# Two-layer graph attention on one core: a row buffer of 41 rows in layer 2, first operands kept in its tail, and TensorE sums for layer 1's largest tile

## The chip, the cores and the metric

The kernel runs on one core of one Trainium2 chip. The metric is device time in microseconds (us) of one execution, the median of several. The engines in the tables are PE (TensorE matmul), PEld (TensorE weight load), DVE (VectorE), ACT (ScalarE), POOL (GpSimd) and SP (SyncE, which here only issues DMAs). All numbers are fp32.

## The reference

10000 nodes carry 768 values each (`x`); 170000 directed edges, 10000 self loops among them, are sorted by destination. Each graph convolution adds one more self loop per node, so that every loop counts twice. Cut to what is computed:

```python
def gat_conv(x, W, a_src, a_dst, bias, heads, concat):
    xl = (x @ W).reshape(n, heads, out_ch)
    e = leaky_relu(a_src_dot(xl)[src] + a_dst_dot(xl)[dst], 0.2)
    e = exp(e - segment_max(e, dst)[dst])
    alpha = e / (segment_sum(e, dst)[dst] + 1e-16)
    return segment_sum(xl[src] * alpha, dst) + bias      # heads joined

h  = relu(layer_norm(gat_conv(x, W1, ..., b1, 4 heads of 256), g1, be1))
h1 = h + (x @ Wr1 + br1)                                  # 1024 columns
h  = layer_norm(gat_conv(h1, W2, ..., b2, 1 head of 768), g2, be2)
out = layernorm(x + h + (h1 @ Wr2 + br2))                 # 768 columns
```

So each node needs, in each layer, a weighted sum over the projected rows of all its neighbours, between two and some forty of them, and then norms and a product that belong to the node alone.

## The kernel before, in words

**Tiles and slots.** A first stage (lines 591 to 659, until about 940 us) multiplies `x` by W1 and writes a row for each node to `table1` in DRAM: 1024 products, four destination and four source logits, and the node's rank. At the same time it sorts the edge lists. The nodes are ordered by degree and cut into 79 tiles of 128. `TURNS` (L97) sets the order in which tiles are handled: every second one, from few neighbours to many, and then the others back down. By position in that order, as the text numbers tiles throughout, tile 0 has 8 rows, the next ones 10, 11, 12, 12, 13, 13, 14; tiles 22 to 24 have 18, 25 to 28 have 19, 29 to 31 have 20, 35 has 22, 38 has 26; tile 39 has 41 and is the largest; then come 27, 25, 24, 23, 22, 22, 21, 21, 20 (tiles 48 to 50), 19 (51 to 53), 18, and so on down to 9 rows in tile 78. A "row" of a tile is the k-th neighbour of each of its 128 nodes: one indirect gather of 128 table rows. There are 1377 rows in each layer. The first row of a tile is the nodes' own, and in layer 2 a plain DMA issued by SP (L452), since table2 is written in the tiles' order; all other rows are gathers issued by POOL (L424).

**The ring.** Class `Ring` (L440) is the row buffer: 29 slots of 1033 columns in layer 1 (`RING1`), 38 of 770 in layer 2 (`RING2`), row q in slot q modulo the size. `fetch(upto)` issues the gathers up to row `upto`; after row q has been used, the kernel calls `fetch(q + 1 + size)`, so that the row that follows in the same slot is asked for. A gather waits on POOL until the last reader of its slot is done.

**Order of the work.** The order of instructions on each engine is the order of the program (`manual_schedule`); the framework only inserts the waits on data and on buffers. Where work of the next tile is to run during the present one, the code says at which row.

**Layer 1** (`ordered_layer1`, L667 to 844, from about 940 to 3437 us). For each tile, `weights_of` (L707) forms the logits and the softmax weights of all rows on DVE and ACT, turns the weights of the first four rows (`ON_PE1`) into diagonal matrices on ACT (L719) and lets PE add these rows to a sum in PSUM (L725). The other rows are added by DVE in `weigh`: one of four as four multiply-adds of 256 columns (L519, "plain"), the others multiplied by ACT (L508) and added by DVE (L515, "shared"). The norm, ReLU and residual follow during the next tile, as do the transposes of the result `h` (L687, L688), the product of x with Wr1 (L171), and `to_layer2` (L796), which stores `h` transposed into `h1_d` (L798), multiplies it by W2 (L803) and has the row of table2 stored (L747). The transposed `x` of a tile also goes to DRAM (`x_d`). A tile that has more rows than the ring has slots cannot be taken so; this is tile 39, with 41 rows for 29 slots. It goes through `attend_parts` (L522): three parts of 13, 14 and 14 rows, each with its own logits, a running maximum with which the sum so far is rescaled, and then the rows, one plain and three shared, each followed by its `fetch`. The end of `attend_parts` divides by the sum of the weights (L427).

**Layer 2** (`ordered_layer2`, L846 to 978). It begins with loads by SP, in this order: Wr2, into the place of Wr1 (L853), the vectors b2, g2, be2, br2 and `shift` (L855 to 857), the own row of tile 0, `h` and `x` of tiles 0 and 1 (`fetch_x`, L864), then the other own rows. `h` and `x` of later tiles use pieces of W2's buffer in turn, two of each. `brT` (L862) is br1 spread over 128 columns, for one product with Wr2 (L952, `product`), which is added to be2 at the end of tile 0 (L973); all rows of this product are the same, so it is a constant vector of the layer's output. For each tile:

- `residual(t)` (L896) adds x (L903) and h times Wr2 (L906) on PE, in PSUM.
- `weights_of(t)` (L877) forms logits and weights, and then ACT makes a diagonal for each row (L891) and PE adds columns 512 to 767 of all rows (L892).
- DVE adds columns 0 to 511 of each row (`weigh`, L965), 0.787 us a row. At row `turn` the logits of the next tile are formed, at `turn + 3` its weights, if that tile's rows fit beside the present one's:

```python
if t + 1 < NT and SLOTS[t + 1] + LEAD <= ring.size:
    ahead = weights_of(t + 1)
    turn = min(max(n // 3, n + SLOTS[t + 1] + 2 * LEAD - ring.size), n - LEAD)
```

- `norms(t)` (L911) runs in steps during the next tile: deviation, scaling and residual (L916, L919), the second norm, and the scatter of the output by POOL (L925).

Tile 39 has 41 rows, and the ring 38 slots: it goes through `attend_parts` in layer 2 too (L946), with all 768 columns on DVE and no work on PE but its residual.

## Time and profile before

| | before |
|---|---|
| median of 3 runs | 5388.15 us |
| lowest and highest | 5386.93, 5388.26 us |
| profiled execution, its own time | 5386.19 us |
| its span in the profile | 5384.3 us |
| granted TensorE clock, mean | 0.941 |
| bytes moved by DMA | 1591.37 MB |
| start of layer 1, of layer 2 (about) | 940 and 3437 us |

The profile is one execution, taken by the hardware profiler. Its span is 1.9 us below the time measured for that same execution, and that is 2.0 us below the median of the runs. The busy time of the engines in the stages, from the windows view (columns: us from the start of the span, busy us of each engine, granted clock, mean busy share of the core's 16 DMA engines, GB/s):

| stage | window | PE | DVE | ACT | POOL | clock | DMA | GB/s |
|---|---|---|---|---|---|---|---|---|
| first stage | 0 to 940 | 863 | 504 | 371 | 460 | 0.97 | 0.43 | 121 |
| layer 1, rising | 940 to 2090 | 1058 | 1030 | 951 | 684 | 0.97 | 0.94 | 344 |
| layer 1, tile 39 | 2090 to 2210 | 44 | 107 | 76 | 61 | 0.67 | 0.65 | 226 |
| layer 1, falling | 2210 to 3437 | 1106 | 1092 | 999 | 691 | 0.96 | 0.91 | 330 |
| layer 2, begin | 3437 to 3600 | 138 | 113 | 58 | 104 | 0.91 | 0.94 | 334 |
| layer 2, rising | 3600 to 4390 | 701 | 661 | 308 | 562 | | | |
| layer 2, tile 39 | 4390 to 4480 | 32 | 71 | 16 | 64 | 0.71 | 0.88 | 285 |
| layer 2, falling | 4480 to 5384 | 779 | 770 | 360 | 612 | 0.92 | 0.90 | 329 |

How to read the lines shown later: in a timeline each line has the start, the length, the engine, the line of the kernel (L12 is line 12), the operation, `out<-in` by the program's names, the shape and the count; in square brackets stands how long the engine was idle before it and which instruction, by engine, released it. Buffers that are parts of another one appear under the larger one's name: in layer 2 `w` is the former buffer of W2 (holding h, x and results), `wr` holds Wr2, `ring` is the row buffer. [...] "Queue" lines (SPq, POOLq) are the issues of DMAs.

### The profile page before, as it was taken

How to read it: one execution, taken by the hardware profiler on the slowest of the kernel's cores; microseconds unless marked ns; L12 is line 12 of the kernel's file. 1: busy time of each engine (PE TensorE's matmuls, PEld its weight loads, DVE VectorE, ACT ScalarE, POOL GpSimd, SP SyncE). 2: the span in 40 equal slices, each digit the busy share in tenths (PEclk: the TensorE clock that was granted, in tenths of full speed). 3: DMA queues.
4: the chain of work that ended last, by engine and by line, in shares of the span. 5: the costliest groups of instructions: out<-in, count | busy, mean ns of one | idle time of the engine just before them, and what ended most of it. 6: DMA issues, size and time to landing. Idle time of an engine off the chain costs nothing. (4 is left out here: it accounts for less than half of the span.)

```text
span 5384.3 us, 59633 instructions
## 1 busy us (share of the span) xinstructions
PE 4721.3 (88%) x15011; PEld 2818.7 (52%) x15011; DVE 4348.2 (81%) x8008; ACT 3138.9 (58%) x8204; POOL 3238.2 (60%) x3159
## 2 busy tenths in 40 slices
PE   8999996999999886478999999799988846889998
PEld 3444443555555543245555555466665534556665
DVE  5784244899999888888999999499887876878998
ACT  3434343787888877778888888344433313334443
POOL 3446455455666665556666554367776766767774
PEclk9999998999999998789999999899998978989999
DMA  4333635899999996899999998699999998999995
GB/s 155 126 98 90 90 93 202 307 338 342 359 358 369 358 346 252 306 323 355 359 365 362 350 334 303 221 327 377 369 337 327 332 301 301 341 328 354 369 382 216
DMA packets 474308, 1591.37 MB, mean 296 GB/s; under 512 B 118327, under 2 KB 122487, under 8 KB 473958
## 3 DMA queue, kind: packets, MB, share of 16 engines
q0 software_dynamic: 322384, 1286.62, 66.3%
q1 hardware_dynamic: 149520, 297.43, 16.3%
q10 hardware_dynamic: 2054, 3.42, 0.2%
q8 instruction: 126, 2.06, 0.2%
q14 instruction: 224, 1.84, 0.1%
HBM read 1431.80 MB, written 177.29 MB: 299 GB/s over the span
## 5 line engine op out<-in xcount | busy, mean ns | idle before, releaser
L424 POOL DMA_INDIRECT ring<-table,slots x2675 | 2659.6, 994 | 1486.7 <-DVE acc L519 366.4
L519 DVE SCALAR_TENSOR_TENSOR acc<-ring,e,acc 128x256 f32<-128x256 f32 (+1 forms) x2538 | 1570.8, 619 | 113.3 <-PE acc L725 37.7
L508 ACT ACTIVATE ring<-ring,e 128x256 f32<-128x256 f32 x3320 | 1351.5, 507 | 0.2
L515 DVE TENSOR_TENSOR acc<-acc,ring 128x1024 f32<-128x1024 f32 x830 | 1021.3, 1230 | 80.6 <-ACT ring L508 9.2
L171 PE MATMUL big<-w,xT 128*128 128x512 f32 x1896 | 826.1, 597 | 27.0 <-DMA w<-in_W_dram 9.6
L906 PE MATMUL big<-wr,w 128*128 128x512 f32 (+1 forms) x2528 | 846.4, 488 | 0.0
L892 PE MATMUL big<-ring,diagonals 128*128 128x256 f32 x2672 | 667.2, 412 | 193.3 <-ACT diagonals L891 180.3
L171 PE MATMUL big<-wr,xT 128*128 128x512 f32 x1896 | 835.4, 597 | 0.2 <-ACT xT L688 0.2
L803 PE MATMUL half<-w,hT 128*128 128x512 f32 (+1 forms) x2528 | 830.4, 486 | 0.0
L892 PEld LDWEIGHTS big<-ring,diagonals 128*128 128x128 f32 x2672 | 548.2, 208 | 309.8 <-ACT diagonals L891 211.8
L803 PEld LDWEIGHTS half<-w,hT 128*128 128x128 f32 x2528 | 477.8, 189 | 372.7 <-issue 310.7
L906 PEld LDWEIGHTS big<-wr,w 128*128 128x128 f32 x2528 | 482.6, 191 | 340.1 <-issue 307.5
L725 PE MATMUL acc<-ring,diagonals 128*128 128x256 f32 x1816 | 452.2, 406 | 220.5 <-ACT diagonals L719 220.2
L171 PEld LDWEIGHTS big<-w,xT 128*128 128x128 f32 x1896 | 362.5, 192 | 486.5 <-issue 467.6
L171 PEld LDWEIGHTS big<-wr,xT 128*128 128x128 f32 x1896 | 357.7, 192 | 421.6 <-issue 420.9
L725 PEld LDWEIGHTS acc<-ring,diagonals 128*128 128x128 f32 x1816 | 365.9, 204 | 299.7 <-ACT diagonals L719 242.7
L891 ACT ACTIVATE diagonals<-ident,e 128x128 f32<-128x128 f32 x1336 | 400.5, 387 | 147.6 <-DVE e L499 129.3
L565 ACT ACTIVATE sd<-mv,eps 128x1 f32<-128x1 f32 x237 | 69.8, 295 | 638.0 <-DVE mv L563 637.7
L649 DVE TENSOR_TENSOR scr<-big,ad_b 128x1024 f32<-128x1024 f32 x79 | 96.7, 1224 | 381.6 <-ACT row L646 381.6
L654 POOL TENSOR_TENSOR row<-row,none 128x1024 f32<-128x1024 f32 x79 | 187.0, 2368 | 266.8 <-ACT row L646 266.3
L719 ACT ACTIVATE diagonals<-ident,e 128x128 f32<-128x128 f32 x908 | 278.5, 387 | 117.6 <-DVE e L499 117.6
L485 ACT ACT_TABLE_LOAD x153 | 196.3, 1283 | 219.7 <-DVE e L484 108.1
(172 smaller groups left out, 3813.4 us busy)
## 6 DMA issues: line engine op xcount, KB each, us to landing
ring<-table,slots POOLq DMA_INDIRECT x2675, 6.9
table<-row SPq DMA_DIRECT2D x79, 516.0 KB, 3.7
h_d<-hT SPq DMA_DIRECT2D x79, 512.0 KB, 6.9
w<-h_d SPq DMA_DIRECT2D x79, 512.0 KB, 8.3
table<-row SPq DMA_DIRECT2D x79, 385.0 KB, 6.4
ring<-table SPq DMA_DIRECT2D x79, 385.0 KB, 6.4
xT<-in_x_cols_dram SPq DMA_DIRECT2D x79, 384.0 KB, 4.5
x_d<-xt SPq DMA_DIRECT2D x79, 384.0 KB, 6.7
```

Source lines behind the costliest of these rows:

```text
L171: nc.tensor.matmul(p[:, c:e], aT[:, j, :], w[:, j, c:e], start=(j == 0), stop=(j == k - 1))
L424: nc.gpsimd.indirect_dma_start(out=to, out_offset=None, in_=table, in_offset=bass.IndirectOffsetOnAxis(ap=index, axis=0), **more)
L485: nc.scalar.activation(e, e, AF.Exp)
L508: nc.scalar.activation(row[:, s], row[:, s], AF.Copy, scale=e[:, h:h + 1])
L515: nc.vector.tensor_add(acc[:, :c], acc[:, :c], row[:, :c])
L519: nc.vector.scalar_tensor_tensor(acc[:, s], row[:, s], e[:, h:h + 1], (acc if first is None else first)[:, s], op0=OP.mult, op1=OP.add)
L719: nc.scalar.activation(diagonals[:, k * H1 + i, :], ident, AF.Copy, scale=e[:, k, i:i + 1])
L725: nc.tensor.matmul(acc[:, c:d], diagonals[:, k * H1 + i, :], ring.slot(FIRST[t] + k)[:, c:d], start=(k == 0 and c % BANK == 0), stop=(k == ...
L803: nc.tensor.matmul(q, hT[:, j, :], w2[:, j, c:c + q.shape[1]], start=(j == 0), stop=(j == K1 - 1))
L891: nc.scalar.activation(diagonals[:, k % G, :], ident, AF.Copy, scale=e[:, k, :])
L892: nc.tensor.matmul(to, diagonals[:, k % G, :], ring.slot(FIRST[t] + k)[:, ON_PE2:C2], start=False, stop=(k == n - 1), skip_group_check=True)
L906: nc.tensor.matmul(r[:, c:d], hT[:, j, :], wr2[:, j, c:d], start=False, stop=(j == K1 - 1 and (d < C2 or not whole(t))), skip_group_check= ...
```

## The change

Two things are changed.

In layer 2 the ring gets 41 slots in place of 38. With 41 slots tile 39 is "whole" and goes the way of all others. The room is found by dropping the separate buffer of `brT`: while the ring is filling, `brT` and the `h` and `x` of tiles 0 and 1 lie at the end of the ring's own buffer (`at_end`, `firsts`), so that the gathers of the last slots wait until they have been read. The loads of SP get the order Wr2, h and x of tile 0, own row of tile 0, `shift`, b2, h and x of tile 1, g2, be2, br2, the other own rows; `shift` and br2 use the same buffer `out` one after the other, and br2 waits for the addition of `shift`. The product of `brT` with Wr2 moves from tile 0's own work to a place ahead of `residual(0)`, the filling of the ring (`ring.fetch(RING2)`) to a place behind `residual(1)`, and the addition of br2 to be2 to the end of tile 0.

In layer 1, tile 39's parts have their first four rows added by PE into PSUM (`summed`, made from the loop of `weights_of`), as other tiles do. DVE adds the first third of the remaining rows plain and the others shared, then the sums from PSUM. The running sum is now the tile `h` in SBUF, not one in PSUM. The rows that follow in the ring are asked for once per part, at its end, not after each row.

```diff
-RING2 = 38
+RING2 = 41
...
-    def attend_parts(small, ring, acc, h_, ad, bias, heads, dh, t):
+    def attend_parts(small, ring, acc, h_, ad, bias, heads, dh, t, summed=None):
...
             top, total = new, part
+            if summed:
+                sums, m = summed(lo, e)
+                for q in range(lo + m, hi):
+                    shared = q >= lo + m + (hi - lo - m) // 3
+                    if shared:
+                        multiply(ring.slot(q), e[:, q - lo], dh)
+                    weigh(acc, ring.slot(q), e[:, q - lo], dh, shared=shared)
+                nc.vector.tensor_add(acc[:, :c], acc[:, :c], sums[:, :c])
+                ring.fetch(hi + ring.size)
+                continue
             for q in range(lo, hi):
...
+            def summed(acc, diagonals, e, q, lo, hi, m):
+
+                for k in range(lo, hi):
+                    for i in range(H1):
+                        nc.scalar.activation(diagonals[:, k * H1 + i, :], ident, AF.Copy,
+                                             scale=e[:, k, i:i + 1])
+                for k in range(lo, hi):
+                    for i in range(H1):
+
+                        c, d = i * DH1, (i + 1) * DH1
+                        nc.tensor.matmul(acc[:, c:d], diagonals[:, k * H1 + i, :], ring.slot(q + k)[:, c:d],
+                                         start=(k == 0 and c % BANK == 0),
+                                         stop=(k == m - 1 and (d % BANK == 0 or d == C1)),
+                                         skip_group_check=True)
...
                 for lo, hi in ((0, min(m, 2)), (min(m, 2), m)):
...
+                    summed(acc, diagonals, e, FIRST[t], lo, hi, m)
                     yield acc
...
                 if live and not whole:
                     due(n)
-                    acc = ps_acc.tile([P, 2 * BANK], F32, name="acc")
+                    sums, acc = (ps_acc.tile([P, 2 * BANK], F32, name="acc") for _ in range(2))
                     ad = small.tile([P, H1], F32, name="ad")
                     nc.vector.tensor_copy(ad, ring.slot(FIRST[t])[:, C1:C1 + H1])
-                    attend_parts(small, ring, acc, acc, ad, None, H1, DH1, t)
+
+                    def some(q, e):
+                        m = min(ON_PE1, e.shape[1])
+                        diagonals = pool.tile([P, ON_PE1 * H1, P], F32, name="diagonals")
+                        summed(sums, diagonals, e, q, 0, m, m)
+                        return sums, m
+
+                    h = pool.tile([P, C1], F32, name="h")
+                    attend_parts(small, ring, h, acc, ad, None, H1, DH1, t, some)
...
-            b2_b, g2_b, be2_b = (spread(pool, v, n, nc.sync)
-                                 for v, n in ((b2, "b2"), (g2, "g2"), (be2, "be2")))
-            adds = [spread(pool, br2, "out", nc.sync), spread(pool, shift, "brT", nc.sync)]
             ring = Ring(pool, table2, R2, RING2, dict(zip(FIRST, TURNS)))
-            ring.fetch(SLOTS[0])
-            nc.vector.tensor_add(be2_b, be2_b, adds[0])
-            nc.vector.tensor_add(b2_b, b2_b, adds[1][:, :C2])
-            brT = spread_br1(pool, "brT")
+
+            rest, flat = RING2 * R2, ring.rows.rearrange("p k n -> p (k n)")
+
+            def at_end(n):
+                nonlocal rest
+                rest -= n
+                return flat[:, rest:rest + n]
+
+            brT = at_end(C1).rearrange("p (k n) -> p k n", n=P)
+            nc.vector.tensor_copy(brT, br1_c[:, :, None].to_broadcast([P, K1, P]))
+            firsts = [(at_end(C1), at_end(D0)) for _ in range(min(2, NT))][::-1]
 
             def fetch_x(t):
 
-                hT, xt = parts[t % 2], parts[2 + t % 2][:, :D0]
+                hT, xt = firsts[t] if t < 2 else (parts[t % 2], parts[2 + t % 2][:, :D0])
                 nc.sync.dma_start(hT, h1_d[t])
                 nc.sync.dma_start(xt, x_d[t])
                 return hT.rearrange("p (k n) -> p k n", n=P), xt
+
+            ins = {0: fetch_x(0)}
+            ring.fetch(SLOTS[0])
+            adds = [spread(pool, shift, "out", nc.sync)]
+            b2_b = spread(pool, b2, "b2", nc.sync)
+            ins[1] = fetch_x(1)
+            g2_b, be2_b = (spread(pool, v, n, nc.sync) for v, n in ((g2, "g2"), (be2, "be2")))
+            nc.vector.tensor_add(b2_b, b2_b, adds[0][:, :C2])
+            adds.append(spread(pool, br2, "out", nc.sync))
+            assert SLOTS[0] <= rest // R2 and NT > 1
...
-            ins = {t: fetch_x(t) for t in range(min(2, NT))}
-            ring.fetch(RING2)
+            q = product(brT, wr2, C2)
             rs = {0: residual(0)}
...
                     if not t:
-                        q = product(brT, wr2, C2)
                         rs[1] = residual(1)
+                        ring.fetch(RING2)
...
                     if not t:
+                        nc.vector.tensor_add(be2_b, be2_b, adds[1])
                         nc.vector.tensor_add(be2_b, be2_b, q[:, :C2])
```

More of the change, by code (lines that the diff above doesn't have):

```diff
@@ L716, in weights_of @@
                 for lo, hi in ((0, min(m, 2)), (min(m, 2), m)):
-                    for k in range(lo, hi):
-                        for i in range(H1):
-                            nc.scalar.activation(diagonals[:, k * H1 + i, :], ident, AF.Copy,
-                                                 scale=e[:, k, i:i + 1])
-                    for k in range(lo, hi):
-                        for i in range(H1):
-                            c, d = i * DH1, (i + 1) * DH1
-                            nc.tensor.matmul(acc[:, c:d], diagonals[:, k * H1 + i, :],
-                                             ring.slot(FIRST[t] + k)[:, c:d],
-                                             start=(k == 0 and c % BANK == 0),
-                                             stop=(k == m - 1 and (d % BANK == 0 or d == C1)),
-                                             skip_group_check=True)
+                    summed(acc, diagonals, e, FIRST[t], lo, hi, m)
                     yield acc
@@ L934, in ordered_layer2 @@
             ready = []
-            assert whole(0) and NT > 1
+            assert whole(0)
             for t in range(NT):
```

## The prediction

> **What bounds the kernel now.** I read the page first: its chain of waits holds only the last 12 us and says nothing, so I go by stages.
>
> ```profile
> span 5384.3 us, 59633 instructions
> PE 4721.3 (88%) x15011; PEld 2818.7 (52%) x15011; DVE 4348.2 (81%) x8008; ACT 3138.9 (58%) x8204; POOL 3238.2 (60%) x3159
> ```
>
> Nothing is full over the whole. The windows view in stretches of 100 us (columns: stretch, its length, busy us of each engine, clock, DMA share, GB/s) shows three holes; the change touches all of them.
>
> ```profile
> 2100.00:2200.00 100.00, 27.91 (x86) 16.11 (x84) 90.21 (x154) 58.67 (x146) 51.42 (x53) 0.65 0.65 224
> 3400.00:3500.00 100.00, 71.16 (x212) 39.58 (x211) 35.43 (x69) 23.61 (x55) 39.69 (x41) 0.85 0.76 274
> 3500.00:3600.00 100.00, 100.00 (x357) 66.34 (x356) 92.35 (x209) 46.37 (x108) 64.08 (x66) 1.00 0.89 321
> 3600.00:3900.00 300.00, 296.29 (x1068) 199.31 (x1066) 270.91 (x585) 131.22 (x310) 222.91 (x231) 1.00 0.99 370
> 3900.00:4300.00 400.00, 335.88 (x1134) 234.11 (x1135) 322.58 (x647) 152.07 (x386) 280.75 (x291) 0.89 0.93 333
> 4400.00:4500.00 100.00, 30.40 (x102) 20.96 (x103) 75.08 (x128) 17.48 (x51) 71.53 (x67) 0.64 0.88 294
> ```
>
> 2100 is layer 1's 41-row tile (number 39 of 79), 3400 the start of layer 2, 4400 layer 2's 41-row tile. After 3600 DMA is full; from 3900, where tiles have 18 rows and more, it is not, and no engine is either: there the loop gather, landing, weights, weighing, free slot sets the pace. The timeline at the start of layer 2 (start, length, engine, line, what, idle before and its releaser):
>
> ```profile
> 3422.43 10.61 PE L803 MATMUL half<-w,hT 128*128 128x512 f32 x32
> 3461.82 2.05 PE L903 MATMUL big<-w,ident 128*128 128x512 f32 x2 [28.78 <-DMA w<-x_d]
> 3475.19 0.17 DVE L477 TENSOR_TENSOR e<-ring,ad 128x10 f32<-128x10 f32 x1 [3.57 <-DMA ring<-table,slots]
> 3491.30 0.95 DVE L973 TENSOR_TENSOR be<-be,big 128x768 f32<-128x768 f32 x1 [9.93 <-PE big L171]
> ```
>
> PE stands still for 28.8 us until tile 0's h and x are there, and DVE 9.9 us for the product of brT. Then a 22-row tile, POOL and DVE:
>
> ```profile
> 4622.18 0.17 DVE L477 TENSOR_TENSOR e<-ring,ad 128x10 f32<-128x10 f32 x1 [5.16 <-DMA ring<-table,slots]
> 4624.40 0.94 POOL L424 DMA_INDIRECT ring<-table,slots  x1 [2.32 <-DVE acc L519]
> ```
>
> The ring is full, POOL waits 2.32 us (0.30 is its usual gap, so 2.0 lost) for a slot, DVE for rows to land. Last, tile 39 in layer 1 and layer 2:
>
> ```profile
> 2132.79 10.51 PE L803 MATMUL half<-w,hT 128*128 128x512 f32 x32
> 2203.43 9.59 PE L725 MATMUL acc<-ring,diagonals 128*128 128x256 f32 x32 [60.13 <-ACT diagonals L719]
> 4446.63 2.05 PE L903 MATMUL big<-w,ident 128*128 128x512 f32 x2 [52.04 <-DMA w<-x_d]
> 4467.53 0.16 DVE L576 RECIPROCAL sd<-sd 128x1 f32<-128x1 f32 x1 [6.40 <-ACT sd L565]
> ```
>
> PE idles 60 and 52 us, but DVE is busy and POOL goes on gathering.
>
> [...]h and x, issued from 3439.7 to 3442.1, share the engines with the gathers and reach PE only at 3461.8. [...]the square root above stood behind 27 diagonals. [...]after the hole 16 matmuls of L906 took 9.12 us, later 7.03.
>
> **A, start of layer 2.** The order of loads becomes h and x of tile 0, own row, shift, b2, h and x of tile 1, the other vectors; tile 0's and 1's h and x land in slots 35 to 40 of the ring, and `product(brT)` goes ahead of `residual(0)` on PE. All of it still waits for the row store that closes layer 1 (issued 3433.5; SP's first load left at 3436.6). Then brT is copied (0.69 us), PE starts near 3437.5 instead of 3461.8, runs the product (10.5) and residual(0) (11.9) by about 3460, when tile 0's weights can begin as before: its eight rows landed at 3460.2, and tile 1's ten at 3475.2, by the pace of DMA. So DVE gets rid of the 9.9, and PE is about 22 us ahead. POOL's gathers of slots 35 to 40 wait for residual 0 and 1 (done by 3480); POOL, at some 1.4 us a gather, comes there at about 3484: hidden; if residual(1) were 10 us late, those 10 us would show. On SP, h and x of tile 2 no longer wait behind the own row in slot 41-38=3, but behind slot 0. What can PE's 22 us buy? From 3600 DMA is full, so no more than its idle time before: 11 us in 3500 to 3600 and 1% of 300 us after, 14 in all. I take **-13**. Ends: -6 (e of tile 2 comes from 3495.8 to 3490 only), and -25 if the last percents of DMA give (it reached 385 GB/s in 5200 to 5300).
>
> **B, 41 rows instead of 38.** `turn` is max(n/3, n+n'+6-ring): for 21 rows and more the limit moves with the ring, and POOL has 6 rows in hand when DVE stops for the next tile's rows, before and after: nothing. Where n/3 rules, the rows in hand grow: 6 to 8 or 9 in seven tiles of 19 and 20 rows (25 to 28, 50 to 52), 6 to 7 in five (29, 30, 47 to 49), and above 7 in the 18s. A row is 1.25 us of POOL (0.95 + 0.30); a stall is 2.0. The 19-row tiles come 26.2 to 27.7 us apart, POOL needs 18x1.25+1.31=23.8. I take 1.5 us for the seven, 0.7 for the five, 0.1 for some ten others: 10.5+3.5+1 = **-15**. Ends: -3 (DMA at 0.93 is nearly full) and -30 (all of POOL's stalls behind `acc` L519 in 3900 to 4300 and 4700 to 5100, 22.5+12.7 us over the gaps, less those of big tiles). In tiles below 18 rows nothing.
>
> **C, tile 39 in layer 2 as a whole tile.** Removed: three parts with 41 additions of 768 columns at 1.02 us (41.8), their logits and fades; added: 41 of 512 at 0.787 (32.3), 41 diagonals on ACT, 41 matmuls. But all 41 rows must now be there before the first weight, and 41+3 > 41, so nothing of it is prepared during tile 38, as before. POOL reaches row 40 about 4400: row 18 goes at 4371.5 (slot freed by the fourth row of tile 38), 22 more x1.25 + a scatter 1.31. With the ring's many padding rows DMA moved 261 to 265 GB/s at 0.96 to 0.98 (4390 to 4410), so 23 rows x0.394 MB /0.28 = 32 us and the landing is at about 4410. DVE, done with tile 38 at 4388.3, waits 22 us, and tile 38's norms wait behind it. Weights at 4413; then 41 diagonals (0.305 each, two thirds held by PE's 0.44 a row) stand before the square root on ACT: it comes near 4427.6, DVE stalls 8.5 us. POOL meanwhile has three free slots, and restarts at 4432; 27 rows of tile 40 go by 4463 and land near 4470, where DVE waits 15 us at `turn`=33; tile 40 starts at 4479.5. Before: 4457.9. That is +21.6; given back: tile 40's weights are then ready, and POOL's stall of 6.9 us at 4465.6 goes. In POOL's own count row 744 leaves at 4484 instead of 4472.5. I take **+12**; ends 0 and +40.
>
> **D, tile 39 in layer 1.** Per part TensorE adds four rows; DVE keeps three plain ones (2.06 each), six or seven shared (1.25), one addition of sums: 12x2.06+29x1.25=61 becomes 9x2.06+20x1.25+3x1.25=47. ACT: 16 diagonals (4.9) and 24 to 28 multiplications (0.40) are the 15 us of before. In part 0 the sums stand behind `to_layer2` on PE (until 2143.3, then 7.6): DVE gets them at 2151, part 0 ends 7 us late. Slots 0 to 3 are free only from 2145, so POOL's refetch starts 18 us later, and the gathers behind follow. The rows of tile 39 it brings first are nearly empty (4 GB/s in 2130 to 2140), tile 40's are full: 24 rows x1.41=34 us of DMA from 2165.5, landing near 2200 to 2203; its weights came at 2199.9. DVE, done by 2195, waits. **+2**, ends -4 and +8. The SBUF accumulator costs nothing beyond a wait for the transposes of h (2122.2), within this.
>
> **Sum.** -13-15+12+2 = -14. The profiled execution took 5386.2 (span 5384.3, 1.9 around it): 5372; the median of the runs is 2.0 above it, so **5374**.
>
> **Rivals.** *DMA has room*: PE's 22 us come through and the stalls go, A -25, B -25, C +8, D +2: -40, 5348. For it, 385 GB/s late in layer 2; against it, 370 at 0.99 and DVE's waits for landing rows. *The two halves cancel*, or the tiles are held by DMA anyway: A -8, B -5, C +12, D +2: +1, 5389; for it, 0.93 in the loose stretch. *Slower*: tile 39 in layer 2, taken whole, costs +40: the landing 6 us later, tile 40's 27 gathers at 1.61 us as many were in 4398 to 4446 (+9), nothing given back (+10), and 3 more behind the diagonals; with A -8, B -15, D +2 that is +19, 5407. With those values of A, B and D (-21) it decides once C exceeds 21 us plus the 11 that can be told, 32. Against it, DVE's 41 additions are 9 us shorter and to PSUM.
>
> **How the numbers follow.** Main case 0.40, DMA has room 0.15, cancel 0.23, slower 0.22. A tenth of the main case lies within 0.2% (11 us, about what a measurement of this kernel tells from none). Faster 0.36+0.14=0.50, same 0.04+0.23=0.27, slower 0.22 and a hundredth of the rest: 0.23. The main case's own range is 5362 to 5384; both signs hold much, so the range goes from 5350 to 5402.
>
> **What would show it.** A: PE's gap after 3433 near 5 us, no wait before L973's successor, DMA share over 0.95 in 3500 to 3600. B: POOL's waits for `acc` in the 19s gone, those tiles near 25 us. C: DVE idle some 20 us before e of 41 columns and 8 before the square root, tile 40 later by 10 to 20. D: tile 40's weights within 5 us of before. It is wrong if the stretch from 3600 to 3900 gets shorter by more than 15 us, if rows of tile 39 land much before 4405, or if the 22-row tiles change.

## The result and the profile after

| | before | after |
|---|---|---|
| median of 5 runs each | 5388.26 us | 5358.83 us |
| lowest to highest | 5386.93 to 5391.10 | 5354.01 to 5363.11 |
| profiled execution, its own time | 5386.19 us | 5358.30 us |
| span in the profile | 5384.3 us | 5356.5 us |

The ratio is 0.9943, with a 95% interval from 0.9932 to 0.9955: about 30 us faster. The forecast was 5374, in a range from 5350 to 5402. Sign and range held, but the change is twice as large as the main case had it, and by the experiments all four parts of its sum were too small, two on the one side and two on the other.

The experiments below came in three groups of four runs. In the first and the third group the kernel before took 5622.64 and 5620.99 us, and every kernel profiled there moved some 300 GB/s in layer 2, while in the second group the kernel before took 5384.22 us, about as here; layer 1 was alike in all three (346 to 347 GB/s on the way up), so layer 1 is read from all runs, and layer 2 from this pair and the second group, with the others compared only inside their group.

The head of the page after:

```profile
span 5356.5 us, 60038 instructions
PE 4759.5 (89%) x15191; PEld 2849.9 (53%) x15191; DVE 4312.2 (81%) x7966; ACT 3150.5 (59%) x8255; POOL 3235.3 (60%) x3159
```

The totals hardly differ. The windows view of the kernel after, in the stretches that the prediction showed (stretch, its length, busy us of PE, PEld, DVE, ACT, POOL, clock, DMA share, GB/s):

```profile
2100.00:2200.00 100.00, 56.58 (x190) 38.42 (x188) 75.17 (x139) 61.50 (x166) 52.65 (x49) 0.81 0.56 200
3400.00:3500.00 100.00, 93.35 (x297) 55.52 (x296) 42.16 (x79) 27.53 (x66) 31.78 (x34) 0.97 0.67 243
3500.00:3600.00 100.00, 96.00 (x325) 61.34 (x324) 91.46 (x207) 47.20 (x110) 75.90 (x79) 0.97 1.00 379
3600.00:3900.00 300.00, 300.00 (x1095) 204.39 (x1094) 283.38 (x605) 137.39 (x329) 225.45 (x234) 1.00 0.99 374
3900.00:4300.00 400.00, 340.17 (x1152) 235.07 (x1151) 329.05 (x663) 155.37 (x394) 289.14 (x302) 0.90 0.95 347
4400.00:4500.00 100.00, 49.58 (x177) 36.87 (x177) 72.17 (x130) 25.82 (x68) 66.80 (x70) 0.73 0.83 285
```

In the tile of 41 rows of layer 1 (2100) DVE is now busy for 75 us instead of 90, yet that is no gain: DMA moves 200 GB/s instead of 224. From 3500 to 3600 DMA moves 379 GB/s where it was 321. From 3900 to 4300 it moves 347 where it was 333.

To place the time, I take from each trace when ACT ends the copy of a tile's table row (layer 1) and when it ends a tile's output (layer 2). "Layer 2" below is the time from the last such row to the last output; the pieces are from output to output. All in us:

| kernel | layer 1, rows of tiles 37 to 78 | layer 2 | to output 37 | 37 to 39 | 39 to 47 | 47 to 60 | 60 to 78 |
|---|---|---|---|---|---|---|---|
| before | 1316.4 | 1938.7 | 940.2 | 101.0 | 251.7 | 323.3 | 322.5 |
| after | 1324.1 | 1900.0 | 900.4 | 117.4 | 256.5 | 302.5 | 323.1 |

Layer 1 lost 7.7 us, all of it around tile 39. Layer 2 won 39.8 us up to output 37, lost 16.4 in tile 39, 4.8 behind it, and won 20.8 in tiles of 20 to 17 rows on the way down. The row of tile 37 in layer 1 came 3.2 us later after than before, ahead of anything that was changed; absolute times around tile 39 are to be compared with that in mind.

Now the lines that answer those of the prediction. The timeline of the kernel after, at the start of layer 2:

```profile
3448.57 12.14 PE L171 MATMUL big<-wr,ring 128*128 128x512 f32 x32 [4.58 <-DVE ring L886]
3470.58 0.17 DVE L477 TENSOR_TENSOR e<-ring,ad 128x8 f32<-128x8 f32 x1 [6.20 <-DMA ring<-table,slots]
3491.64 0.95 DVE L1008 TENSOR_TENSOR be<-be,big 128x768 f32<-128x768 f32 x1
```

PE begins 4.6 us after its last product of layer 1, with the product of brT, where it stood for 28.8 us. Tile 0's logits still wait for their rows. The addition to be2 has no wait ahead of it, where there were 9.9 us.

Layer 1's tile 39: the first gather that refills the ring, in the timeline of the kernel before,

```profile
2127.15 0.99 POOL L424 DMA_INDIRECT ring<-table,slots  x1 [2.65 <-DVE acc L519]
```

and in that of the kernel after, with what follows:

```profile
2149.09 0.98 POOL L424 DMA_INDIRECT ring<-table,slots  x1 [22.36 <-PE acc L728]
2154.06 1.22 DVE L553 TENSOR_TENSOR h<-h,acc 128x1024 f32<-128x1024 f32 x1 [10.33 <-PE acc L728]
2209.92 0.18 DVE L477 TENSOR_TENSOR e<-ring 128x20 f32<-128x20 f32 x1 [4.80 <-DMA ring<-table,slots]
```

POOL stands for 22.4 us until PE has added the first row of part 0, DVE 10.3 us for the sums. The gathers begin 21.9 us later on the clock, 18.7 without the 3.2 us from ahead of the change. The last logits of tile 40 are formed at 2209.9, where it was 2199.9 before.

Layer 2's tile 39, same view:

```profile
4372.67 0.22 DVE L477 TENSOR_TENSOR e<-ring,ad 128x35 f32<-128x35 f32 x1 [13.11 <-DMA ring<-table,slots]
4382.20 0.17 DVE L477 TENSOR_TENSOR e<-ring,ad 128x6 f32<-128x6 f32 x1 [9.31 <-DMA ring<-table,slots]
4400.34 0.16 DVE L587 RECIPROCAL sd<-sd 128x1 f32<-128x1 f32 x1 [11.40 <-ACT sd L576]
4441.36 0.20 DVE L477 TENSOR_TENSOR e<-ring,ad 128x27 f32<-128x27 f32 x1 [13.75 <-DMA ring<-table,slots]
```

DVE waits 22.4 us for the 41 rows, 11.4 for a square root behind the 41 diagonals on ACT, 13.8 for tile 40's 27 rows.

### The profile page after: what moved, and what is told of

The parts are those of the page before. It is cut to its first block, busy times and chain, and to the rows that moved or that the text cites. A ratio compares the mean times of both kernels' runs of the same rounds, so it can differ in the third digit from the quotient of the medians.

```text
span 5356.5 us, 60038 instructions
## 1 busy us (share of the span) xinstructions
PE 4759.5 (89%) x15191; PEld 2849.9 (53%) x15191; DVE 4312.2 (81%) x7966; ACT 3150.5 (59%) x8255; POOL 3235.3 (60%) x3159
## 3 DMA queue, kind: packets, MB, share of 16 engines
q1 hardware_dynamic: 149520, 297.43, 16.4%
## 5 line engine op out<-in xcount | busy, mean ns | idle before, releaser
L519 DVE SCALAR_TENSOR_TENSOR acc<-ring,e,acc 128x512 f32<-128x512 f32 (+1 forms) x2530 | 1577.6, 624 | 113.3 <-PE acc L728 37.8
L508 ACT ACTIVATE ring<-ring,e 128x256 f32<-128x256 f32 x3284 | 1337.1, 507 | 0.0
L515 DVE TENSOR_TENSOR acc<-acc,ring 128x1024 f32<-128x1024 f32 x801 | 985.5, 1230 | 78.4 <-ACT ring L508 9.7
L927 PE MATMUL big<-ring,diagonals 128*128 128x256 f32 x2754 | 683.2, 410 | 208.4 <-ACT diagonals L926 189.7
L941 PE MATMUL big<-wr,w 128*128 128x512 f32 (+1 forms) x2464 | 824.2, 488 | 0.0
L927 PEld LDWEIGHTS big<-ring,diagonals 128*128 128x128 f32 x2754 | 561.8, 207 | 327.2 <-ACT diagonals L926 229.9
L728 PE MATMUL acc<-ring,diagonals 128*128 128x256 f32 x1912 | 476.3, 406 | 208.1 <-ACT diagonals L722 207.7
L941 PEld LDWEIGHTS big<-wr,w 128*128 128x128 f32 x2464 | 470.1, 191 | 330.5 <-issue 298.7
L171 PEld LDWEIGHTS big<-w,xT 128*128 128x128 f32 x1896 | 362.9, 192 | 487.2 <-issue 468.4
L728 PEld LDWEIGHTS acc<-ring,diagonals 128*128 128x128 f32 x1912 | 385.0, 204 | 291.9 <-ACT diagonals L722 232.3
L926 ACT ACTIVATE diagonals<-ident,e 128x128 f32<-128x128 f32 x1377 | 411.1, 387 | 138.8 <-DVE e L499 129.7
L722 ACT ACTIVATE diagonals<-ident,e 128x128 f32<-128x128 f32 x956 | 292.8, 387 | 116.2 <-DVE e L499 115.9
```

Source lines behind the costliest of these rows:

```text
L171: nc.tensor.matmul(p[:, c:e], aT[:, j, :], w[:, j, c:e], start=(j == 0), stop=(j == k - 1))
L508: nc.scalar.activation(row[:, s], row[:, s], AF.Copy, scale=e[:, h:h + 1])
L515: nc.vector.tensor_add(acc[:, :c], acc[:, :c], row[:, :c])
L519: nc.vector.scalar_tensor_tensor(acc[:, s], row[:, s], e[:, h:h + 1], (acc if first is None else first)[:, s], op0=OP.mult, op1=OP.add)
L722: nc.scalar.activation(diagonals[:, k * H1 + i, :], ident, AF.Copy, scale=e[:, k, i:i + 1])
L728: nc.tensor.matmul(acc[:, c:d], diagonals[:, k * H1 + i, :], ring.slot(q + k)[:, c:d], start=(k == 0 and c % BANK == 0), stop=(k == m - 1 ...
```

## The experiments

The question is which part brings what, and by which mechanism. Each kernel below leaves out, adds or moves one part of the change. Medians are in us, ratios are to the kernel before in the same group.

### The start alone, and where the product of brT stands

`start_only` is the kernel before with the new start of layer 2 and nothing else, `ring38` the changed kernel with 38 slots:

```diff
-RING2 = 41
+RING2 = 38
```

(`start_only` has these 38 slots too, and besides layer 1's tile 39 as before.) `product_late` is the changed kernel with one line moved:

```diff
-            q = product(brT, wr2, C2)
             rs = {0: residual(0)}
...
                     if not t:
+                        q = product(brT, wr2, C2)
                         rs[1] = residual(1)
```

`product_first` is the kernel before with the opposite move, its loads left in the old order:

```diff
+            q = product(brT, wr2, C2)
             rs = {0: residual(0)}
...
                     if not t:
-                        q = product(brT, wr2, C2)
                         rs[1] = residual(1)
```

Expected of `start_only`:

> Layer 1 as before, the ring of layer 2 with 38 slots as before; only the new start of layer 2 (brT, h and x of tiles 0 and 1 in the ring's tail, order of loads, product of brT ahead of residual 0). Theory 1: TensorE sets the pace until tiles of 16 or 17 rows (it was 100% busy from 3500 to 3880 us), so its 22 to 24 us of earlier start come through whole: 5388 - 22 = 5366, and output 21 is 20 us earlier than before. Theory 2 (the prediction): DMA sets it, so no more than its 14 idle us: 5374 or more, output 21 no more than 14 us earlier.

Of `ring38`:

> The changed kernel with 38 slots in layer 2 in place of 41 (so its tile 39 goes through the parts again, in three). What is left is the new start of layer 2 and layer 1's sums. Theory 1: the start is worth TensorE's lead of 22 us, the slots the rest of what layer 2 wins up to output 37: layer 2 is 22 us shorter than before, the whole 22 - 9.5 = 12 us faster than before. Theory 2: the start is worth all 40 us up to output 37: 30 us faster than before. Where transfers are slower in layer 2, as on the chip of the runs before (290 to 320 GB/s), both give less, 5 to 10 us.

Of `product_late`:

> The changed kernel with the product of brT where it was, in tile 0's own work behind its weights, while h and x of tiles 0 and 1 are still loaded first into the ring's tail. Theory 1 (TensorE sets the pace of the first tiles): TensorE stands idle until tile 0's weights and runs the product's 10.5 us afterwards: layer 2 is 10 us longer than the changed kernel's. Theory 2 (DMA sets it): 0 to 4 us longer.

Of `product_first`:

> The kernel before with the product of brT ahead of residual 0 on TensorE, nothing else: all loads in the old order. TensorE can run the product before h and x of tile 0 are there, and is some 9 us ahead of before from tile 1 on. Theory 1: what cost the kernel before some 20 us at the start is that TensorE's late diagonals (and the vector engine's 9.9 us for the product) hold slots that POOL waits for (5.7, 4.5, 3.4, 1.3 and 2.0 us between 3500 and 3600): 12 to 18 us faster. Theory 2: the early loads of h and x are what counts: 0 to 4 us faster.

| kernel | group | median | ratio | 95% interval | layer 2 | to output 21 |
|---|---|---|---|---|---|---|
| before | this pair | 5388.26 | | | 1938.7 | 487.2 |
| `ring38` | 2 | 5374.94 | 0.9982 | 0.9976 to 0.9989 | 1918.3 | 466.7 |
| `product_late` | 2 | 5354.35 | 0.9949 | 0.9932 to 0.9966 | 1901.4 | 468.8 |
| after | this pair | 5358.83 | 0.9943 | 0.9932 to 0.9955 | 1900.0 | 465.8 |
| `start_only` | 1 | 5614.15 | 0.9989 | 0.9977 to 1.0000 | 2146.3 | 519.4 |
| `product_first` | 3 | 5617.38 | 0.9991 | 0.9980 to 1.0003 | 2172.5 | 527.9 |

The start is worth 20.4 us of layer 2 (`ring38` against before), all of it by output 21; in its median 9.3 are left, since layer 1's sums take a part. `start_only` is 8.5 us faster by the medians, at 300 GB/s and with an interval that just reaches no change, and so has neither theory's number. In the second group the number is near that of theory 1, PE's lead.

`product_late` was to tell the theories apart, and does not. Its PE runs the product 31 us later than in the changed kernel, and comes to residual 1 ten us later (45.6 us behind the end of layer 1 instead of 35.3). Its timeline on PE:

```profile
3448.13 2.05 PE L938 MATMUL big<-ring,ident 128*128 128x512 f32 x2 [8.96 <-DMA ring<-table]
3474.83 10.48 PE L171 MATMUL big<-wr,ring 128*128 128x512 f32 x32
```

But the changed kernel does not keep those ten us. Its PE stands still ahead of residual 3, until x of tile 3 has landed, and `product_late` has no such wait:

```profile
3517.77 2.05 PE L938 MATMUL big<-w,ident 128*128 128x512 f32 x2 [4.00 <-DMA w<-x_d]
```

At residual 4 `product_late` is only 3.3 us behind the changed kernel, at output 21 it is 3.0 behind, and its layer 2 is 1.4 us longer (5.1 longer than in `early_sums`, which has the same layer 2 as the changed kernel and ran in the same group). So the place of the product is worth a few us at most, which fits the second theory's 0 to 4, and fits the first one too once only 3.3 us are left of the ten.

Does PE set the pace there, or DMA? I go by the starts of the residuals. Residual 22 begins 341 to 342 us after residual 4 in this pair and in all four kernels of the second group, and PE shows at most 0.7 us of idle time between them. Up to output 21 PE's idle time falls from 32 us (before) to 11 (`ring38`), which is as much as layer 2 gains. That speaks for PE. On the other side `last_rows_parts`, whose start is the same, comes to residual 4 another 4.0 us sooner than the changed kernel and is at output 21 only 0.2 us sooner; and DMA is at a share of 0.98 to 0.99 all the while. Which of the two holds the tiles after 3600 is not shown.

What the traces do show is how the gathers fare up to there. I compare POOL's long waits in the timeline. Before:

```profile
3504.39 0.94 POOL L424 DMA_INDIRECT ring<-table,slots  x1 [5.71 <-DVE sd L919]
3521.14 0.94 POOL L424 DMA_INDIRECT ring<-table,slots  x1 [4.47 <-PE big L892]
3538.32 0.94 POOL L424 DMA_INDIRECT ring<-table,slots  x1 [3.36 <-PE big L892]
```

They go on with 1.30, 2.12 and 1.99 up to 3600: 19 us in six waits, four of which end with PE. From 3500 to 3600 no wait of POOL is longer than 0.9 us in `ring38`, nor longer than 1.3 in `product_late`. A row's slot is free when DVE and PE have read it, PE through the diagonals of columns 512 to 767. In the kernel before PE is so late that in those four waits it, and not DVE, frees the slot. `product_first` was meant to show this from the other side and did not: its 0.9991 can't be told from no change. But it says why. PE began the product there only 21 us after its last product of layer 1, with h and x about to land, and residual 2 began 73.1 us behind the end of layer 1, where it is 74.4 before, 62.3 in `product_late` and 52.0 after. PE had gained nothing by then, and the waits stayed (timeline of POOL in `product_first`):

```profile
3510.98 0.94 POOL L424 DMA_INDIRECT ring<-table,slots  x1 [4.50 <-PE big L892]
3528.84 0.94 POOL L424 DMA_INDIRECT ring<-table,slots  x1 [4.88 <-PE big L892]
```

So with early loads and the product in its old place nearly all of the gain is there (`product_late`), and with the product first and the old loads none can be told. That points to the early loads of h and x. The other parts of the new start (the order of the vectors, the place of `ring.fetch`, the late addition of br2) were not separated from them.

How can DMA carry more, if it was full? The windows view from output 0 to output 5, of the kernel before:

```profile
3508.50:3590.50 82.00, 82.00 (x285) 52.88 (x283) 75.56 (x175) 35.73 (x79) 54.30 (x56) 1.00 0.92 329
```

and of `ring38`:

```profile
3508.50:3588.50 80.00, 80.00 (x292) 54.18 (x291) 74.99 (x172) 35.49 (x80) 60.48 (x63) 1.00 1.00 375
```

The engines' busy share rises from 0.92 to 1.00, but the bytes from 329 to 375 GB/s. By bytes, with 374 as full, before lost 82 x (1 - 329/374) = 9.9 us here and 75 x (1 - 330/374) = 8.8 ahead of output 0; `ring38` lost nothing here and 65.9 x (1 - 353/374) = 3.7 ahead. That is 15 of the 20.4 us; the rest is in the stretch from output 5 to 21, which ran at 368 GB/s before and at 374 in `ring38`. Both kernels moved the same bytes up to output 21 (173 MB, rate times time). So this account says where the time went; it doesn't say what held the rate.

### The slots, and tile 39 in layer 2

`no_sums` is the changed kernel with layer 1's tile 39 as before, `ring41_parts` the same with `whole(t)` as `SLOTS[t] < ring.size`. `tile39_parts` is the changed kernel with that edit alone:

```diff
-                return SLOTS[t] <= ring.size
+                return SLOTS[t] < ring.size
```

`slots_only` is the kernel before with 41 slots, the separate buffer of brT kept, and tile 39 in parts:

```diff
-RING2 = 38
+RING2 = 41
...
-                return SLOTS[t] <= ring.size
+                return SLOTS[t] < 41
```

With 41 slots `attend_parts` makes two parts of tile 39, with 38 it made three. Expected of `no_sums` and `ring41_parts`:

> The changed kernel with layer 1's tile 39 as before (no TensorE sums, fetch after each row). Theory 1: the sums cost what layer 1's end shows, 9.5 us, and nothing makes it up later: 5359 - 9.5 = 5349. Theory 2 (the prediction): they cost 2 us, and the rest of the later end of layer 1 is chance: 5357.

> As no_sums, but layer 2's tile 39 goes through the parts again (two parts of 20 and 21 rows with a ring of 41). Theory 1: taking tile 39 whole cost the 16 us between outputs 37 and 39, for good: 5349 - 16 = 5333. Theory 2: the 15 us that the changed kernel wins between outputs 43 and 54 are the other side of those 16 (transfers that ran while the vector engine stood), so that without the one there is less of the other: 5345 to 5350.

Of `tile39_parts` and `slots_only`:

> The changed kernel with layer 2's tile 39 sent through the parts (two of 20 and 21 rows), nothing else. Theory 1: taken whole it costs 15 to 18 us for good: the changed kernel's layer 2 minus 15 to 18, 5338 where before is 5386. Theory 2: the time comes back in the tiles behind: within 5 us of the changed kernel.

> The kernel before with 41 slots in layer 2 and nothing else: brT keeps its own buffer, the start is the old one, tile 39 goes through the parts (two with 41 slots). Theory 1: the slots alone take away the vector engine's waits for landing rows (31 us between outputs 47 and 60 of the kernel before, 10 with 41 slots and the new start), whatever the start is: layer 2 shorter by 30 to 40 us. Theory 2: the slots count only behind the new start, which fills them: 15 us or less (my prediction's size too).

| kernel | group | median | ratio | 95% interval | layer 2 | 37 to 39 |
|---|---|---|---|---|---|---|
| `no_sums` | 1 | 5646.38 | 1.0047 | 1.0030 to 1.0064 | 2204.7 | 126.3 |
| `ring41_parts` | 1 | 5620.72 | 0.9997 | 0.9981 to 1.0013 | 2164.3 | 108.0 |
| `tile39_parts` | 3 | 5621.36 | 1.0000 | 0.9986 to 1.0015 | 2157.4 | 101.5 |
| `slots_only` | 3 | 5627.97 | 1.0005 | 0.9992 to 1.0018 | 2168.3 | 108.5 |

These are the groups in which layer 2 moved 300 GB/s. Inside the first group one thing is clear: tile 39 taken whole costs 18 us from output 37 to 39, and 26 in the median (`no_sums` against `ring41_parts`). There the whole of the new layer 2 is a loss. `slots_only` can't be told from before: with transfers at that rate the slots bring nothing measurable by themselves. What they would bring alone at the usual rate was not measured, so theory 2 of that run is neither shown nor refuted. `tile39_parts` ends where the kernel before does (1.0000), but no changed kernel ran beside it, so its own time doesn't decide between its theories; `last_rows_parts` below does that.

In the second group the slots can be read against `ring38`, behind the new start:

| kernel | layer 2 | to output 37 | 37 to 39 | 39 to 47 | 47 to 60 | 60 to 78 |
|---|---|---|---|---|---|---|
| `ring38` (38 slots, tile 39 in three parts) | 1918.3 | 919.5 | 101.4 | 250.7 | 323.3 | 323.5 |
| `early_sums` (41, whole) | 1896.3 | 903.8 | 115.2 | 254.7 | 299.5 | 323.3 |
| `last_rows_parts` (41, two parts) | 1881.3 | 905.2 | 96.4 | 255.6 | 301.8 | 322.4 |

(The last two differ from the changed kernel in layer 1 besides, see below.) The three slots win 14 to 16 us up to output 37 and 22 to 24 between outputs 47 and 60, where tiles have 20 to 17 rows, and lose 4 to 5 behind tile 39, whether it is taken whole or not. Of what is won behind output 47, 18 to 19 us lie in the six tiles of 20 and 19 rows, up to output 53, and 3 to 5 in the seven of 18 and 17. The list of waits on DVE (engine, line, operand, what was waited for: us in total, times, longest) between outputs 47 and 60, of `ring38`:

```profile
DVE e L477 <- DMA ring<-table,slots: 31.1, 10, 4.8
```

of `last_rows_parts`:

```profile
DVE e L477 <- DMA ring<-table,slots: 10.5, 8, 3.7
```

and of the kernel before and the one after, in turn:

```profile
DVE e L477 <- DMA ring<-table,slots: 31.0, 10, 5.1
```

```profile
DVE e L477 <- DMA ring<-table,slots: 11.8, 9, 3.3
```

The wait for landing rows shrinks by 20.6 us, and the stretch by 21.5. The landing itself takes about as long as before (median 6.6 us from issue in this stretch of `ring38`, 6.8 in that of `last_rows_parts`). By the order of the program three more slots mean that the last row of the next tile is asked for three rows, 2.4 us of weighing, earlier. POOL's waits for rows that DVE has yet to use shrink too, in the same list of `ring38` and of `last_rows_parts`:

```profile
POOL ring L424 <- DVE acc L519: 22.6, 37, 3.9
```

```profile
POOL ring L424 <- DVE acc L519: 15.0, 37, 2.2
```

Less the usual gap of 0.30 us each, that is 11.5 us of stalls in the one and 3.9 in the other.

Up to output 37 the wait for landing rows doesn't shrink: from output 24 to 37 it is 54.8 us in `ring38` and 59.2 in `last_rows_parts`. But other waits of DVE do: 6.7 us put down to a scatter of the output and 5.5 put down to nothing, both ahead of logits, are there in `ring38` alone, and 2.8 us for square roots are gone. All waits of DVE together fall from 70.0 to 59.4 us, and the stretch from 377.9 to 367.4. Some 4 us are won at output 37 alone, where tiles have 24 and 26 rows.

### Layer 1's tile 39

`sums_only` is the kernel before with layer 1's sums. `early_sums` moves the products for layer 2 behind the sums of part 0:

```diff
                 if live and not whole:
+                    behind = [event for event in events if event[1] is to_layer2]
+                    events = [event for event in events if event[1] is not to_layer2]
                     due(n)
...
                         summed(sums, diagonals, e, q, 0, m, m)
+                        while behind:
+                            behind.pop()[1]()
```

`last_rows_parts` has that too, lets PE add the last four rows of a part, and fetches behind each of the other rows (and takes layer 2's tile 39 in parts):

```diff
-                for q in range(lo + m, hi):
-                    shared = q >= lo + m + (hi - lo - m) // 3
+                for q in range(lo, hi - m):
+                    shared = q >= lo + (hi - lo - m) // 3
                     if shared:
                         multiply(ring.slot(q), e[:, q - lo], dh)
                     weigh(acc, ring.slot(q), e[:, q - lo], dh, shared=shared)
+                    ring.fetch(q + 1 + ring.size)
...
-                        summed(sums, diagonals, e, q, 0, m, m)
+                        n = e.shape[1] - m
+                        summed(sums, diagonals, e[:, n:], q + n, 0, m, m)
```

`last_rows_42` is the same with 42 slots in layer 2 (tile 39 still in two parts). Expected of them:

> The kernel before with layer 1's tile 39 changed alone. Theory 1: 9.5 us later from tile 39 on, at the end too: 5388 + 9.5 = 5398. Theory 2 (the prediction): +2, 5390.

> The changed kernel, with the TensorE sums of part 0 of layer 1's tile 39 ahead of the products for layer 2 (to_layer2), not behind them. Theory 1: the sums stand 10.3 us behind these products, and the slots of the first four rows come free as much later, so that tile 40's rows land 10 us late: layer 1 ends 10 us earlier than in the changed kernel, total -10. Theory 2: the fetch once per part is what makes the rows late, not where the sums stand: layer 1 ends within 3 us of the changed kernel's.

> As early_sums, and TensorE adds the last four rows of a part in place of the first four, the others being followed each by its fetch again; layer 2 has 41 slots but takes tile 39 through the parts (two). Theory 1: gathers start with the first weighed row (some 2131 us by the clock of the changed profile in place of 2149), layer 1 ends 5 to 10 us earlier than before the change, 15 to 20 earlier than in the changed kernel; layer 2 is shorter than the changed kernel's by the 16 us of tile 39. Together 31 to 36 us below the changed kernel. Theory 2: the landing of tile 40's rows is held by DMA whatever the order: layer 1 ends as before the change (10 below the changed kernel), and layer 2 gives back what tile 39 saves: 10 to 15 below the changed kernel.

> As last_rows_parts, with 42 slots in layer 2[...]. Theory 1: what a slot brings shrinks with the waits that are left (10.5 us for landing rows between outputs 47 and 60 of last_rows_parts): layer 2 another 5 to 8 us shorter, 5310. Theory 2: at 41 slots DMA is the limit everywhere (0.98 from output 50 on): within 3 us of last_rows_parts.

| kernel | group | median | ratio | 95% interval | layer 1, tiles 37 to 78 |
|---|---|---|---|---|---|
| `sums_only` | 1 | 5628.66 | 1.0017 | 1.0004 to 1.0030 | 1325.5 |
| `early_sums` | 2 | 5345.22 | 0.9929 | 0.9912 to 0.9945 | 1312.6 |
| `last_rows_parts` | 2 | 5317.53 | 0.9873 | 0.9856 to 0.9889 | 1312.1 |
| `last_rows_42` | 3 | 5612.38 | 0.9986 | 0.9973 to 1.0000 | 1310.8 |

The six traces without the sums have 1316.4 to 1319.5 us in the last column, mean 1318.6; the five with the sums as changed have 1323.6 to 1326.5, mean 1325.1. The sums cost 6.5 us, without overlap between the two sets.

`early_sums` gives back those and six more. Its timeline on PE has the two blocks in the new order:

```profile
2134.53 7.09 PE L728 MATMUL acc<-ring,diagonals 128*128 128x256 f32 x32
2141.45 10.51 PE L816 MATMUL half<-w,hT 128*128 128x512 f32 x32
```

POOL's first gather follows the first added row (2136.7 instead of 2149.1), and the last logits of tile 40 are formed about as much earlier (2198.2 instead of 2209.9):

```profile
2136.69 1.43 POOL L424 DMA_INDIRECT ring<-table,slots  x1 [11.88 <-PE acc L728]
2198.19 0.18 DVE L477 TENSOR_TENSOR e<-ring 128x20 f32<-128x20 f32 x1 [4.82 <-DMA ring<-table,slots]
```

That is theory 1: the sums themselves are a gain, and their place behind `to_layer2` turns it into a loss. Fetching once per part stayed as it was, so it isn't what makes the loss. `last_rows_parts` has its first gather at 2128.8 and the last logits at 2193.5, 4.7 us earlier still, but at the end of layer 1 only 0.5 of them are left: theory 2's side of that run, the tiles behind take the time back. Its layer 2 is 15 to 19 us shorter than in `early_sums` and the kernel after, where tile 39 is taken whole, and theory 1 holds there. DVE's two waits that remain around its tile 39:

```profile
4411.32 0.20 DVE L477 TENSOR_TENSOR e<-ring,ad 128x27 f32<-128x27 f32 x1 [3.35 <-DMA ring<-table,slots]
4425.32 0.16 DVE L588 RECIPROCAL sd<-sd 128x1 f32<-128x1 f32 x1 [7.37 <-ACT sd L577]
```

11 us instead of 48. At 0.9873 this version beats both kernels: 66.7 us faster than before in its group, some 36 faster than the changed kernel (0.9943 of 5384.22 is 5353.5).

`last_rows_42` falls into the third group. Its layer 1 is as good as that of the last; what a slot more brings to layer 2 at the usual rate of transfers stays open.

## Why the prediction was right, and where it was wrong

The sign was right, and so were the steps of C and D. In A the order of events was right and the ceiling on the gain too low; in B the direction was right and the account of its size was not. The sum is half of what was measured. That it isn't further off is luck: the errors of its parts have different signs.

| part | predicted | shown | from |
|---|---|---|---|
| A, start of layer 2 | -13 | -20 | `ring38` against before |
| B, 41 slots | -15 | -33 | pieces of layer 2 outside 37 to 39, three kernels with 41 slots and the one after, against `ring38` |
| C, tile 39 whole in layer 2 | +12 | +15 | 37 to 39: 115.2, 115.7 and 117.4 against 101.0 and 101.4 |
| D, layer 1's sums | +2 | +6.5 | mean of five traces with the sums against six without |
| sum | -14 | -32 | the profiles differ by 27.9, with after 3.2 late ahead of the change |

**A.** What was to be seen was seen: a gap of 4.6 us on PE, no wait ahead of the addition to be2, DMA at 1.00 from 3500 to 3600, and the gathers of slots 35 to 40 without a wait longer than 0.64 us. The step that failed is "From 3600 DMA is full, so no more than its idle time before: 11 us in 3500 to 3600 and 1% of 300 us after, 14 in all". It took busy time for bytes. At a share of 0.89 the stretch moved 321 GB/s, 14% below the 374 of 3600 to 3900 after the change (the stretch itself then moved 379, with no wait of POOL longer than 0.62 us); and what was lost ahead of 3500 was left out. The term measured 20. PE was 22 us ahead at residual 2, as forecast, but x of tile 3 then came late, and at residual 4 some 15 were left. Whether those 15 us of PE or the bytes of DMA set the size of the gain stays open.

**B.** The step that failed is "A row is 1.25 us of POOL; a stall is 2.0. (...) I take 1.5 us for the seven, 0.7 for the five, 0.1 for some ten others". The mis-sized term is what a tile gains. POOL's stalls do shrink, as the step had it, but over outputs 47 to 60 by 7.6 us, while DVE's wait for landing rows shrinks by 20.6 and the stretch by 21.5. The six tiles of 20 and 19 rows up to output 53 win 18 to 19 us, where the step adds up to 6. It also put nothing on tiles of 21 rows and more, and some 4 us come at output 37. The far end of B (-30, all of POOL's stalls) was near the size, and DVE's waits for landing rows stood in the rival as a reason against a larger gain. The rival "DMA has room", with A and B at -25 each, was the nearer case for layer 2.

**C.** The mechanism was right step by step: 22.4 us until the 41 rows are there (predicted 22), 11.4 for the square root (8.5), 13.8 for tile 40's rows (15). Off was only what comes back: +21.6 less some 10 was taken, and +15 was left. Against two parts in the same ring of 41 slots (96.4) it costs 19 to 21. The gathers of 1.61 us that the slower case counted on did not come: the 35 from 4404 to 4450 in the kernel after, beside DVE's additions to PSUM and its wait for tile 40's rows, took 0.94 to 0.98 us each; the 28 from 4398 to 4441 in the kernel before, beside additions to SBUF, took 0.94 to 1.74, 1.21 on average.

**D.** Also right in its steps: the sums stand behind `to_layer2`, part 0 ends late, the gathers start 18.7 us later (predicted 18; without the 3.2 us from ahead of the change), and tile 40's rows come late. The mis-sized term is the landing, "near 2200 to 2203": the logits came at 2209.9, or 2206.7 without the 3.2. The 39 gathers from the first refill to the last row of tile 40 took 1.13 us each on average, and up to 2.1, instead of the 0.99 of the kernel before, which adds 5.6 us; the last of them went out at 2205.2 and landed at 2209.9. The sum in SBUF cost DVE itself nothing: 1225 ns an addition of 1024 columns, where it was 1233 to PSUM. Whether the longer gathers beside it come from its place was not shown.

That the range held is owed to its ends, not to the middle. The chance of a slower kernel, 0.23, rested on tile 39 at +40 and was answered by +15; at 300 GB/s, where the slots by themselves brought nothing measurable, the same changed layer 2 did end slower (`no_sums`, 1.0047).

## What to carry to other kernels

Size a stretch that DMA sets by its bytes against the best rate seen nearby (here 321 against 374 GB/s), not by its busy share (0.89), and ask which reader frees a buffer last: when one of two readers falls behind the other, the transfers into that buffer wait for it (here POOL for PE, up to 4.5 us at a time). An experiment that delays one engine tells little until it is known how much of the delay is left where the pace is set: here 3 of 10 us were. When a ring is made larger, count how much earlier the last row of the next tile is asked for, and compare that with the consumer's wait for its landing. Work moved to an idle engine must not only fit there: if it frees buffers, it must stand ahead of work that nobody waits for: here POOL stood for 22.4 us until PE had added its first row, and for 11.9 with the sums placed first.

## What was not expected of the hardware

The DMA engines showed a busy share of 0.92 at 329 GB/s and of 0.99 to 1.00 at 374 to 379 in the same loop. The rate of layer 2 itself is not fixed: in two of three groups the kernel before took some 235 us longer than here, and the traces of `start_only` and `slots_only` show 276 to 336 GB/s in layer 2 at shares of 0.80 to 0.93, with layer 1 at its usual rate (352 GB/s in a long stretch of `start_only`, 354 in the same one before). One of these groups ran on the same chip as the group at the usual rate. No run shows the cause, which would have to spare layer 1; it is left open.
